# Attention with sinks: both tiles' scores in a row, their products two slots later, and the PSUM banks dealt out as four, two and two

## The chip, the core and the metric

The program runs on one core of one Trainium2 chip. The metric is the device time of one execution in microseconds (us), taken as the median of the runs. The engines go by the names of the profile: PE is TensorE (its weight loads are PEld), DVE is VectorE, ACT is ScalarE, POOL is GpSimd, SP is SyncE. Each engine takes its own queue of instructions in order; engines wait for one another by semaphores.

## The reference

Sixteen layers of a model follow one another on a tensor of 16 sequences, 256 tokens and 128 channels. The change concerns one layer, `L2_attn_b`, an attention with sinks followed by a mixture of experts, and of it only the attention:

```python
q = apply_interleaved_rope(q, cos, sin) * SCALE      # 16 heads of 64
k = apply_interleaved_rope(k, cos, sin) * SCALE      # 4 heads of 64, repeated 4 times
scores = jnp.einsum('bquh,bkuh->buqk', q, k)
scores = jnp.where(jnp.abs(pos[:, None] - pos[None, :]) <= 128, scores, NEG)
combined = jnp.concatenate([scores, sink], axis=-1)  # one sink per head
probs = softmax(combined)[..., :-1]
out = jnp.einsum('buqk,bkuh->bquh', probs, v)
return jnp.einsum('buqh,uhm->bqm', out, Wo) + bo
```

An RMS norm stands before it and another behind it.

## The kernel before

All 4096 tokens lie in SBUF with channels on the partitions, in 8 chunks of 512 tokens (two sequences each). `window_attention` is one stage of the program; its work is written out by hand in a loop over slots `n`, and the instructions of each engine keep the order in which this loop names them.

A *unit* is `(c, side, b, it, jt)`: chunk, half of the heads, sequence, tile of 128 queries, tile of 128 keys. There are 128 units, 16 per chunk, 8 per side. The two units of one query tile (`jt` 0 and 1) follow each other; I call them a pair. A side has four pairs, and the work of a pair takes two slots, a double slot. The steps, in the order in which a unit passes them:

- `prepare` (with `roped` and `moved`) makes the queries and keys of a side while the units of the side before run. For each of five parts (k, and four groups q0 to q3 of 512 columns) PE projects into a bank, ACT evicts it with its bias into `raw`, POOL multiplies by the sine (`t2`); one double slot later `moved` multiplies `raw` by the cosine and shuffles `t2` on DVE (L3191, L3192), and POOL adds the two. The first double slot of a side projects k and q0, the second q1 and q2, the third q3, the fourth none. In the third and fourth of every other side the chunk's values are made as well (`v`).
- `score`: PE multiplies keys by queries for two half sets of heads into two banks, on 64 rows of the array each; ACT takes the exponential into `pt`.
- `masked`: for unequal tiles DVE multiplies `pt` by the mask `far`; at the second unit of a pair POOL adds the pair's two `pt` into `both`.
- `weigh` (L3259): PE multiplies the weights by the values, 8 matmuls per unit on 32 columns of the array each, into the bank `po`, and at the second unit `both` by ones into the bank `pd`, which gives the sums.
- `inverse` and `divide`: ACT takes Ln of the sums with the sinks added and Exp of minus that (`rd`); DVE multiplies `po` by `rd` into `ot`.
- `out`: PE multiplies a finished side's `ot` by the output weights, four matmuls into one bank; DVE adds the result to `h` (`ha` in the profile).
- `before` and `after` are the norms of a chunk, spread over three slots each: a matmul for the mean, one for the variance, then scaling on DVE.

The loop puts `score(n)` at the head of slot n, then `masked(n - 1)` and what earlier slots left over for now (`due`: `inverse` one slot behind the products, `divide` one behind that, and the maxima `peaks`). An odd slot ends with `weigh` of units n - 3 and n - 2. An even slot ends with `prepare`, then `out`, then `before` and `after`; `prepare` begins with `moved`, and so the rotation of q3 stands in front of `out` in DVE's queue:

```python
if n % 2:
    for i in (n - 3, n - 2):
        if 0 <= i < len(units):
            weigh(i, n)
    continue
i, step = divmod(n + 8, 8)
if 0 <= i < 2 * NCH:
    prepare(i, step // 2, n)
i, rest = divmod(n - 14, 8)
if rest == 0 and 0 <= i < 2 * NCH:
    out(i)
```

The eight PSUM banks are dealt out by `share(s=4, o=4)`: four, taken in turn, for scores, projections, values, `out` and norms; four for the pairs `po` and `pd`, so that two pairs' sums can stand at once. Matmuls and the helpers `act`, `tt`, `gt` have one line each (L504, L528, L531 on DVE, L534 on POOL), so groups are told apart by the tiles' names.

Of the kernel before, what the change touches and what calls it, by code (L numbers as in the profile page):

```python
# [11 lines left out]
F32, BF16, I32 = mybir.dt.float32, mybir.dt.bfloat16, mybir.dt.int32  # L12
# [5 lines left out]
P = 128  # L18
# [3 lines left out]
NCH = NT // CH  # L22
# [1627 lines left out]
class Fast(Net):  # L1650
# [1509 lines left out]
    def window_attention(self, w, h, n1, ns2):  # L3160
# [3 lines left out]
        with ExitStack() as st:  # L3164
            p1 = self.stage(st, "w1", 1)
# [11 lines left out]
            def roped(n, g, s, t1):  # L3177


                pa = self.bank("s")  # L3180
                self.mm(pa, w["W" + n][:, g * P : g * P + P], n1[:, s])
                raw = p2.tile([P, CH], F32, tag="raw", name="raw", bufs=4)
                t2 = p2.tile([P, CH], F32, tag="t2", name="t2", bufs=4)
                self.act(raw, pa, AF.Identity, bias=w["b" + n][:, g : g + 1])
                self.gt(self.bt(t2), self.bt(raw), self.twice(w["sin"]), ALU.mult)
                pending.append((t1, raw, t2))
# [8 lines left out]
            def later(slot, f, *args):  # L3195
                due.setdefault(slot, []).append((f, args))

            def prepare(i, step, slot):

                c, side = divmod(i, 2)  # L3200
                s = self.chunk(c)
                while pending:
                    moved()
                if step == 0:
                    qs[i] = p2.tile([P, 4, CH], F32, tag="q", name="q")
                    ks[i] = p2.tile([P, CH], F32, tag="k", name="k")
                    roped("k", side, s, ks[i])
                    later(("last", slot + 4), self.peak, WINDOW + side, 1, c, ks[i])
                for g in ((0,), (1, 2), (3,), ())[step]:
                    roped("q", 4 * side + g, s, qs[i][:, g])  # L3210
                    later(("last", slot + 4), self.peak, WINDOW + side, 0, 4 * c + g, qs[i][:, g])
                if side == 0 and step > 1:
                    pv = self.bank("s")
                    v = p1.tile([P, 2, T], F32, tag="v", name="v", bufs=4)
                    for k in range(2):
                        t = 2 * step - 4 + k
                        self.mm(pv[:, k * T : k * T + T], n1[:, c * CH + t * P : c * CH + t * P + P], w["Wv"])
                        vs[c, t] = v[:, k]
                    self.tt(v, self.bt(pv), w["bv"][:, None, :].broadcast_to([P, 2, T]), ALU.add)
# [14 lines left out]
            def masked(n):  # L3234

                c, side, b, it, jt = units[n]
                if it != jt:
                    pp = pts[n].rearrange("p r h t -> p (r h) t")
                    self.tt(pp, pp, w["far"][:, it * P : it * P + P][:, None, :].broadcast_to([P, 8, P]), ALU.mult)
                if jt:  # L3240
                    both[n] = p2.tile([P, 2, 4, P], F32, tag="both", name="both")
                    self.gt(both[n], pts[n - 1], pts[n], ALU.add)

            def weigh(n, slot):
                c, side, b, it, jt = units[n]
                if jt == 0:
                    sums[0] = self.bank("o"), self.bank("o")
                pt = pts.pop(n)
                po, pd = sums[0]


                for dh in range(3 if jt else 2):
                    if dh == 2:
                        pt = both.pop(n)
                    for r in range(4):
                        half, hh = divmod(r, 2)
                        d = (2 * side + half) * 64 + 32 * dh
                        at = dh % 2 * T
                        nc.tensor.matmul(  # L3259
                            (pd if dh == 2 else po)[32 * r : 32 * r + 32, at : at + T],  # L3260
                            self.ones64[:, :32] if dh == 2 else vs[c, 2 * b + jt][:, d : d + 32],
                            pt[:, half, 2 * hh : 2 * hh + 2].rearrange("p h t -> p (h t)"),
                            start=dh == 2 or (jt == 0 and dh == 0), stop=dh == 2 or (jt == 1 and dh == 1), skip_group_check=True,
                        )
                if jt:
                    later(slot + 1, inverse, n, po, pd, slot + 2)

            def inverse(n, po, pd, slot):
                side = units[n][1]
                rd = p2.tile([P, 2, P], F32, tag="rd", name="rd")  # L3270
                for h2 in range(2):
                    self.act(rd[:, h2], pd[:, h2 * P : h2 * P + P], AF.Ln, bias=es[:, side, h2 : h2 + 1])
                self.act(rd, rd, AF.Exp, scale=-1.0)
                later(slot, divide, n, po, rd)

            def divide(n, po, rd):
                c, side, b, it, jt = units[n]
                if (b, it) == (0, 0):
                    ots[2 * c + side] = p2.tile([P, 4, CH], F32, tag="ot", name="ot")
                i0 = b * T + it * P  # L3280
                self.tt(
                    ots[2 * c + side][:, :, i0 : i0 + P].rearrange("p (d h) t -> p d h t", d=2),
                    po.rearrange("p (d h t) -> p d h t", d=2, h=2), rd[:, None].broadcast_to([P, 2, 2, P]), ALU.mult,
                )

            def out(i):
                c, side = divmod(i, 2)
                pz = self.bank("s")
                ot = ots.pop(i)
                for g in range(4):  # L3290
                    at = (4 * side + g) * C
                    self.mm(pz, w["Wof"][:, at : at + C], ot[:, g], start=g == 0, stop=g == 3)
                hs = h[:, self.chunk(c)]
                if side:
                    self.tt(hs, hs, pz, ALU.add)
                else:
                    self.stt(hs, pz, w["bo"], hs, ALU.add, ALU.add)

            held = {}

            def before(c, i):

                s = self.chunk(c)
                if i == 0:
                    held["sq"] = self.centre_step(p1, self.x[:, s], h[:, s], "s", square=True)
                elif i == 1:
                    held["rs"] = self.spread_step(p1, held["sq"], "s", twice=True)
                else:
                    r1, r2 = held["rs"]
                    self.stt(n1[:, s], h[:, s], w["ns1"], r2, ALU.mult, ALU.mult)  # L3310
                    self.tt(h[:, s], h[:, s], r1, ALU.mult)

            def after(c, i):

                s = self.chunk(c)
                if i == 0:
                    held["sq"] = p1.tile([P, CH], F32, tag="nsq", name="nsq", bufs=2)
                    self.act(held["sq"], h[:, s], AF.Square)
                elif i == 1:
                    held["rs"] = self.spread_step(p1, held["sq"], "s")  # L3320
                else:
                    self.stt(n1[:, s], h[:, s], ns2, held["rs"], ALU.mult, ALU.mult)

            with self.share(s=4, o=4), self.tc.manual_schedule():
                self.logs()
                for n in range(-14, len(units) + 16):
                    if 0 <= n < len(units):
                        score(n)
                        later(n + 1, masked, n)
                    for f, args in (*due.pop(n, []), *due.pop(("last", n), [])):  # L3330
                        f(*args)
                    if n % 2:
                        for i in (n - 3, n - 2):
                            if 0 <= i < len(units):
                                weigh(i, n)
                        continue
                    i, step = divmod(n + 8, 8)
                    if 0 <= i < 2 * NCH:
                        prepare(i, step // 2, n)
                    i, rest = divmod(n - 14, 8)  # L3340
                    if rest == 0 and 0 <= i < 2 * NCH:
                        out(i)
                    c, u = divmod(n + 14, 16)
                    if u in (0, 2, 4) and c < NCH:
                        before(c, u // 2)
                    c, u = divmod(n - 24, 16)
                    if u in (0, 2, 4) and 0 <= c < NCH:
                        after(c, u // 2)
# [459 lines left out]
```

## Time and profile before

| what | value |
|---|---|
| median of 3 runs | 4373.4 us (4373.02 to 4376.56) |
| profiled execution | 4392.96 us, span 4391.2 us, mean granted PE clock 0.952 |
| whole span, busy: PE, DVE, ACT, POOL | 90%, 59%, 54%, 48% |
| the attention's stretch | about 3028 to 3500 us |
| in 3028 to 3500, busy us of 472: PE, DVE, ACT, POOL | 448.8, 381.1, 271.7, 412.4; clock 0.99 |

Busy PE is an upper reading: matmuls are pipelined and their ends are modelled, and the instructions of row tiles and column tiles run beside each other. In the timeline each row gives the start and the time of one or several instructions in a row; in brackets stands the idle time of the engine before them and what ended it. Durations overlap a little (a row's end lies up to 0.1 us behind the next row's start on the same engine), so steps are better read from start to start. A wait for several things is put down to the one that came last.

### The profile page before, as it was taken

What the parts mean: (1) busy time and instruction counts of PE and PEld (TensorE: products, weight loads), DVE (VectorE), ACT (ScalarE), POOL (GpSimd) and SP (SyncE); (2) the same over time, 40 slices, a digit from 0 to 9 for tenths busy, and PEclk for the clock granted to TensorE, in tenths of its full rate; (3) what the DMA queues carried; (4) which work ended last, traced back from release to release, by engine and by line L of the source; (5) the groups of instructions that cost most, each with busy time, mean ns of one, the idle gap of its engine ahead of it and who ended that gap; (6) DMA issues with size and microseconds to landing.
All of it is one profiled execution on the core that took longest, in us unless ns stands there. A gap on an engine that the chain in (4) does not pass through costs nothing. (4 is left out here: it accounts for less than half of the span.)

```text
span 4391.2 us, 72802 instructions
## 1 busy us (share of the span) xinstructions
PE 3966.2 (90%) x28390; PEld 2202.4 (50%) x28390; DVE 2605.3 (59%) x4455; ACT 2376.1 (54%) x4549; POOL 2119.4 (48%) x1776
## 2 busy tenths in 40 slices
PE   7899999999899999995989969887999899899978
PEld 3455455466355445543975549643333344355333
DVE  4764566364366377456336643564888788386374
ACT  6665466444766456553447634445555554675442
POOL 4653355232455255315433334466998789521251
PEclk8999999999999999997999979998999999999989
DMA  1800000000000000001940029200000000000000
GB/s 59 332 1 1 11 1 1 19 1 1 19 1 1 1 3 1 1 0 49 310 162 10 15 88 326 86 18 16 1 1 1 3 1 1 15 2 18 6 0 20
DMA packets 78400, 176.36 MB, mean 40 GB/s; under 512 B 12606, under 2 KB 39108, under 8 KB 77920
## 3 DMA queue, kind: packets, MB, share of 16 engines
q1 hardware_dynamic: 65568, 148.40, 9.8%
q0 software_dynamic: 9120, 18.51, 1.2%
q8 instruction: 227, 3.72, 0.4%
q10 hardware_dynamic: 3360, 4.72, 0.3%
q14 instruction: 125, 1.02, 0.1%
HBM read 118.28 MB, written 54.20 MB: 39 GB/s over the span
## 5 line engine op out<-in xcount | busy, mean ns | idle before, releaser
L528 ACT ACTIVATE pt<-ps 128x512 f32<-128x512 f32 (+1 forms) x896 | 423.1, 537 | 408.1 <-PE ps L504 406.8
L504 PE MATMUL ps<-hb,w 128*128 128x512 f32 (+1 forms) x960 | 468.9, 623 | 5.4 <-issue 3.3
L531 DVE TENSOR_TENSOR t<-ps,tab 128x512 f32<-128x512 f32 x512 | 319.3, 683 | 196.1 <-ACT sq L528 191.3
L504 PE MATMUL ps<-w,hb 128*128 128x512 f32 (+2 forms) x896 | 415.1, 576 | 13.6 <-DVE t L531 11.3
L534 POOL TENSOR_TENSOR t<-t,ss 128x1024 f32<-128x1024 f32 x128 | 243.7, 1904 | 306.8 <-ACT ss L528 197.7
L534 POOL TENSOR_TENSOR t<-t,t 128x512 f32<-128x512 f32 x256 | 320.5, 1275 | 13.2 <-PE ps L504 10.1
L504 PEld LDWEIGHTS ps<-hb,w 128*128 128x128 f32 (+1 forms) x960 | 183.6, 196 | 273.5 <-issue 247.3
L531 DVE TENSOR_TENSOR u<-u,ps 128x384 f32<-128x384 f32 (+1 forms) x206 | 121.8, 595 | 277.8 <-ACT u L528 131.2
L534 POOL TENSOR_TENSOR nsq<-ha 128x512 f32<-128x512 f32 x112 | 123.2, 1100 | 314.1 <-ACT ha L528 297.3
L504 PE MATMUL ps<-nsq,ct 128*128 128x512 f32 x368 | 209.5, 654 | 53.9 <-POOL nsq L534 35.0
L528 ACT ACTIVATE pt<-pt 128x768 f32<-128x768 f32 (+1 forms) x160 | 169.5, 1060 | 154.6 <-DVE pt L531 154.6
L2199 POOL DMA_INDIRECT back<-y,x x142 | 139.1, 980 | 184.2 <-ACT y L528 90.2
L504 PE MATMUL ps<-qkt 64*128 64x192 f32 (+1 forms) x2048 | 216.2, 326 | 11.8 <-ACT pt L528 11.8
L504 PE MATMUL ps<-u,w 128*128 128x512 f32 (+1 forms) x448 | 218.8, 612 | 8.0 <-POOL u L534 8.0
L504 PE MATMUL ps<-ot,w 128*128 128x512 f32 x448 | 211.1, 604 | 15.2 <-POOL ot L534 6.9
L504 PE MATMUL ps<-xt,w 128*128 128x128 f32 x1704 | 219.8, 279 | 1.5 <-ACT xt L528 1.5
L504 PEld LDWEIGHTS ps<-qkt 64*128 64x128 f32 x2048 | 153.1, 188 | 133.3 <-ACT qkt L528 51.5
L504 PEld LDWEIGHTS ps<-w,hb 128*128 128x128 f32 x896 | 147.4, 192 | 139.4 <-issue 110.7
L531 DVE TENSOR_TENSOR pt<-ps,w 128x384 f32<-128x384 f32 (+1 forms) x320 | 171.2, 576 | 75.6 <-PE ps L504 72.2
L3705 POOL DMA_INDIRECT rows<-out,idx x128 | 126.4, 988 | 174.6 <-ACT out L528 125.6
L528 ACT ACTIVATE u<-ps,w 128x512 f32<-128x512 f32 x160 | 107.2, 685 | 186.3 <-PE ps L504 183.5
L531 DVE TENSOR_TENSOR pt<-pt,w 128x1024 f32<-128x1024 f32 (+1 forms) x96 | 181.1, 1886 | 42.3 <-ACT pt L528 42.3
(362 smaller groups left out, 9127.2 us busy)
## 6 DMA issues: line engine op xcount, KB each, us to landing
w<-in_moe_x SPq DMA_DIRECT2D x142, 533.0 KB
rows<-t SPq DMA_DIRECT2D x64, 520.0 KB
x<-rows SPq DMA_DIRECT2D x142, 65.0 KB
w<-in_local_f SPq DMA_DIRECT2D x8, 659.5 KB
y<-back ACTq DMA_DIRECT2D x16, 256.0 KB
y<-back SPq DMA_DIRECT2D x16, 256.0 KB
w<-in_local_f SPq DMA_DIRECT2D x4, 658.5 KB
back<-y,x POOLq DMA_INDIRECT x142
```

The source lines that it names most:

```text
L504: self.nc.tensor.matmul(out, lhsT, rhs, start=start, stop=stop)
L528: self.nc.scalar.activation(out, in_, func, **kw)
L531: self.nc.vector.tensor_tensor(out, a, b, op)
L534: self.nc.gpsimd.tensor_tensor(out, a, b, op)
L2199: nc.gpsimd.indirect_dma_start(views[i], bass.IndirectOffsetOnAxis(ap=x[:, C : C + 1].bitcast(I32), axis=0), y, None, bounds_check=2 * NT ...
L3705: nc.gpsimd.indirect_dma_start(views[(c * 2 + k) * 4 + t], bass.IndirectOffsetOnAxis(ap=idx[:, k, t : t + 1], axis=0), out[:, k, t], None,)
```

## The change

The loop goes by double slots. Each one scores both units of a pair in a row, masks the pair of the double slot before, and multiplies the pair of two double slots before (`weigh(n - 4)`, `weigh(n - 3)`; it was units n - 3 and n - 2 of an odd slot n). Then come the maxima, `out`, `prepare`, and `inverse`, which now holds the division as well and belongs to the pair multiplied in the same double slot; `before` and `after` close it. `out` now stands in front of `prepare`. The banks are dealt out as four for scores, two for `po` and `pd`, and two (`f`) for all the rest.

```diff
-                pa = self.bank("s")
+                pa = self.bank("f")
...
-            def weigh(n, slot):
+            def weigh(n):
...
-                if jt:
-                    later(slot + 1, inverse, n, po, pd, slot + 2)
-
-            def inverse(n, po, pd, slot):
+                sums[n] = po, pd
+
+            def inverse(n):
+                po, pd = sums.pop(n)
                 side = units[n][1]
                 rd = p2.tile([P, 2, P], F32, tag="rd", name="rd")
                 for h2 in range(2):
                     self.act(rd[:, h2], pd[:, h2 * P : h2 * P + P], AF.Ln, bias=es[:, side, h2 : h2 + 1])
                 self.act(rd, rd, AF.Exp, scale=-1.0)
-                later(slot, divide, n, po, rd)
-
-            def divide(n, po, rd):
                 c, side, b, it, jt = units[n]
...
-            with self.share(s=4, o=4), self.tc.manual_schedule():
+            with self.share(s=4, o=2, f=2), self.tc.manual_schedule():
                 self.logs()
-                for n in range(-14, len(units) + 16):
-                    if 0 <= n < len(units):
-                        score(n)
-                        later(n + 1, masked, n)
-                    for f, args in (*due.pop(n, []), *due.pop(("last", n), [])):
+                for n in range(-14, len(units) + 16, 2):
+                    two = (n, n + 1)
+                    for i in two:
+                        if 0 <= i < len(units):
+                            score(i)
+                    for i in two:
+                        if 0 <= i - 2 < len(units):
+                            masked(i - 2)
+                    for i in (n - 4, n - 3):
+                        if 0 <= i < len(units):
+                            weigh(i)
+                    for f, args in due.pop(("last", n), []):
                         f(*args)
-                    if n % 2:
-                        for i in (n - 3, n - 2):
-                            if 0 <= i < len(units):
-                                weigh(i, n)
-                        continue
+                    i, rest = divmod(n - 14, 8)
+                    if rest == 0 and 0 <= i < 2 * NCH:
+                        out(i)
                     i, step = divmod(n + 8, 8)
                     if 0 <= i < 2 * NCH:
                         prepare(i, step // 2, n)
-                    i, rest = divmod(n - 14, 8)
-                    if rest == 0 and 0 <= i < 2 * NCH:
-                        out(i)
+                    if 0 <= n - 3 < len(units):
+                        inverse(n - 3)
                     c, u = divmod(n + 14, 16)
```

`out`, the values and the norms' matmuls take their banks from `f` in the same way as `roped`. The number of tiles `pt` (six) and `both` (two) is as it was.

More of the change, by code (lines that the diff above doesn't have):

```diff
@@ L3212, in prepare @@
                 if side == 0 and step > 1:
-                    pv = self.bank("s")
+                    pv = self.bank("f")
                     v = p1.tile([P, 2, T], F32, tag="v", name="v", bufs=4)
@@ L3240, in masked @@
                 if jt:
-                    both[n] = p2.tile([P, 2, 4, P], F32, tag="both", name="both")
+                    both[n] = p2.tile([P, 2, 4, P], F32, tag="both", name="both", bufs=2)
                     self.gt(both[n], pts[n - 1], pts[n], ALU.add)
-            def weigh(n, slot):
+            def weigh(n):
                 c, side, b, it, jt = units[n]
@@ L3287, in out @@
                 c, side = divmod(i, 2)
-                pz = self.bank("s")
+                pz = self.bank("f")
                 ot = ots.pop(i)
@@ L3304, in before @@
                 if i == 0:
-                    held["sq"] = self.centre_step(p1, self.x[:, s], h[:, s], "s", square=True)
+                    held["sq"] = self.centre_step(p1, self.x[:, s], h[:, s], "f", square=True)
                 elif i == 1:
-                    held["rs"] = self.spread_step(p1, held["sq"], "s", twice=True)
+                    held["rs"] = self.spread_step(p1, held["sq"], "f", twice=True)
                 else:
@@ L3319, in after @@
                 elif i == 1:
-                    held["rs"] = self.spread_step(p1, held["sq"], "s")
+                    held["rs"] = self.spread_step(p1, held["sq"], "f")
                 else:
                     self.stt(n1[:, s], h[:, s], ns2, held["rs"], ALU.mult, ALU.mult)
-            with self.share(s=4, o=4), self.tc.manual_schedule():
+            with self.share(s=4, o=2, f=2), self.tc.manual_schedule():
                 self.logs()
-                for n in range(-14, len(units) + 16):
-                    if 0 <= n < len(units):
-                        score(n)
-                        later(n + 1, masked, n)
-                    for f, args in (*due.pop(n, []), *due.pop(("last", n), [])):
-                        f(*args)
-                    if n % 2:
-                        for i in (n - 3, n - 2):
-                            if 0 <= i < len(units):
-                                weigh(i, n)
-                        continue
+                for n in range(-14, len(units) + 16, 2):
[10 more added lines that the diff above has]
+                    for f, args in due.pop(("last", n), []):
+                        f(*args)
+                    i, rest = divmod(n - 14, 8)
+                    if rest == 0 and 0 <= i < 2 * NCH:
+                        out(i)
                     i, step = divmod(n + 8, 8)
```

## The prediction

> **What bounds the kernel now.** The page names no single bound: the last chain holds 3% for PE, and the work is a row of stages. The change touches one of them, so I read that stage by its own rows. It runs from about 3028 to 3500 us of the span: 472 of 4391 us. First the stretches, in columns of start:end and length, then busy us (instructions) of PE, PE's weight loads, DVE, ACT and POOL, then granted clock and DMA:
>
> ```profile
> 3195.00:3224.00 29.00, 27.78 (x216) 11.27 (x213) 23.85 (x30) 14.78 (x32) 26.17 (x15) 1.00 0.01 1
> 3224.00:3253.00 29.00, 28.12 (x215) 11.01 (x214) 24.31 (x32) 18.79 (x41) 25.92 (x14) 1.00 0.00 1
> ```
>
> PE is at 96%, POOL at 90%, DVE at 83%, the clock is full and DMA is nothing. PE looks like the bound. The waits of the stage and the order of time say otherwise:
>
> ```profile
> ACT pt L528 <- PE ps L504: 188.2, 84, 6.4
> PEld ps L3259 <- POOL both L534: 21.9, 16, 3.5
> PE ps L3259 <- POOL both L534: 14.2, 16, 3.0
> PE ps L504 <- POOL q L534: 7.7, 14, 1.0
> ```
>
> PE waits for POOL 14 times for `q`, 1.0 us at most: once in every side. ("ACT pt" waits long because ScalarE has little to do.) The timeline (start, duration, engine, line, instruction) shows the place; weight loads and ACT are left out:
>
> ```profile
> 3289.44 3.70 PE L504 MATMUL ps<-ot,w 128*128 128x512 f32 x8
> ...
> 3291.84 1.15 DVE L531 TENSOR_TENSOR q<-raw,w 128x512 f32<-128x512 f32 x1
> 3292.40 2.82 POOL L534 TENSOR_TENSOR both<-pt 128x1024 f32<-128x1024 f32 x1
> ...
> 3292.92 0.74 DVE L3192 STREAM_SHUFFLE t<-t 128x512 f32<-128x512 f32 x1
> 3293.07 1.13 PE L504 MATMUL ps<-q,k 64*128 64x512 f32 x4
> 3293.55 0.67 DVE L531 TENSOR_TENSOR ha<-ha,ps 128x512 f32<-128x512 f32 x1
> ...
> 3295.18 1.72 POOL L534 TENSOR_TENSOR q<-q,t 128x512 f32<-128x512 f32 x1
> ...
> 3296.95 1.13 PE L504 MATMUL ps<-q,k 64*128 64x512 f32 x4 [0.46 <-POOL q L534]
> ```
>
> The first scores of a side need the fourth part of its queries (q3), which is rotated one double slot earlier: cosine product and shuffle on DVE, sum on POOL. At present DVE does q3 (3291.84) while the `ot,w` matmuls of `out` run, and adds `out`'s result after it (3293.55). POOL then finishes q3 at 3296.90, just too late. Going back, POOL has worked without a gap since the `both` that began at 3275.46: 21.5 us (22.4 us in the neighbouring side). So the loop of a side is PE's first scores and projections, exponentials and mask (7.7 us), then POOL's row (21.5 to 22.4). The `out` matmuls repeat every 59.45 us for two sides (3200.88 to 3260.33), 29.7 per side. PE's own sum below is 28.35.
>
> **The change, part by part.** I call the four double slots of a side A (k and q0 are projected), B (q1, q2), C (q3) and D (`out`; values too in every other side).
>
> *PE's order.* It was score, projections, score, products; it becomes both scores, products, projections. The steps from start to start in the rows: one score 1.06, both in a row 1.92 (a run of eight score instructions, 3475.78 to 3477.70), products 2.30, two projections 1.92, three 2.77, `out` 3.63 and 0.85 for values. Before: A 2x1.06+2.30+1.92 = 6.34, B 7.19, C 6.34, D 8.05 (+0.43 mean for values) = 28.35. After, with 1.92 for 2.12: 27.55. That is 0.8 us per side, 12 us over 15 sides. It counts only where PE binds.
>
> *Products two slots later.* `both` is ready nearly a slot before its products; the 36 us of waits for it (21.9+14.2, largely PE and its loads counted twice) go. Late next is what follows.
>
> *ACT's and DVE's order.* In a double slot ACT now does four exponentials, the slot's `raw` evictions, and behind them Ln, Ln, Exp of the same slot's sums; DVE does mask, peaks, `out`'s add, rotations, values, and last the division. The listing of the changed kernel's instructions shows just this order on DVE in D: mask, two peaks, add to `ha` (waits for PE), q3's product, shuffle, division. So q3, which the next scores need, is queued behind `out`'s matmuls. POOL's order is unchanged.
>
> *Banks: four for scores as before, two for sums (were four), two for the rest.* The next products must now wait for the division before them. Row first: products to Ln 2.43 (3495.43 to 3497.86), Ln to division 1.11 (3299.09 to 3300.20), division 0.60: 4.14 from the start of the products, 1.84 past their end. The scores in between take 1.92, so with nothing in the way the wait is nothing; with `raw` and rotations in the way it is what the timeline below gives, 0.9 to 1.5 per side.
>
> [...]
>
> *Two banks for the rest.* B and the D of half the sides use more; the third matmul of B needs q1's eviction, 1.17+0.57 = 1.74 after the start, and comes up at 1.7: nothing.
>
> **One side, worked through.** 0 is when POOL has finished q3. From the rows: a matmul's reader starts 0.43 per instruction + 0.32 after its start (3490.74 to 3494.47 for `out`); raw 0.57; DVE mask 1.14 to 1.61, peak 0.6, q product 1.08, shuffle 0.62, k product 0.61, values and `out` add 0.6.
> - A: scores to 1.92, products to 4.22, k and q0 to 6.14. Raw of q0 6.25 to 6.82, Ln to Exp 7.93, division 8.53.
> - B: scores to 8.06; products wait 0.5 for the division, 8.55 to 10.85; projections to 13.6. Raw of q2 ends 13.45, division 15.16. DVE's mask of B stands behind A's division and ends at 9.7 to 10.1; then POOL's row begins.
> - C: scores to 15.5, products to 17.8, projections to 19.7. DVE: mask 16.8, peaks 18.0 (q0 is summed by 16.6), q1 19.7, q2 21.4, values 22.0 in every other side, division 22.0 or 22.6.
> - D: scores to 21.6; products wait 0.4 or 1.0, 22.05 or 22.65 to 24.35 or 24.95; `out`'s reader 3.73 later, 28.1 or 28.7; add, q3's product and shuffle 2.3 more: 30.4 or 31.0; POOL's sum 1.26 (alone) to 2.25 (rows), 1.7 taken (the 3295.18 row): 32.1 or 32.7.
>
> The side takes 32.4 by this path. POOL's own path agrees: 9.9 + 21.5 to 22.4 = 31.4 to 32.3. Against 29.7 that is +2.7 us. `out` and q3 meet in D in 14 slots (the changed kernel's and the present one's `ot,w` rows with projections behind them: 3082.50 to 3467.74): 14x2.7 = 38. At the stage's start, PE now waits up to 3.0 for `both`, which goes, while the divisions cost about as much: 0. At its end the last two pairs of products, now back to back, stand in row for the division: +2. Sum +40. The next stage needs this one's output, so it all counts. Profiled execution: 4392.96+40 = 4433; the median of the runs lies 19.6 lower, 4373.4+40 = 4413.
>
> Bounds: no wait for a division at all and POOL's sum at 1.26 gives A 6.14 + B 6.99 + C 6.14 + D 1.92+2.30+3.73+2.3+1.26 = 30.8, +1.1 per side, +15: 4389. Upwards, DVE's q product takes 2.2 and the mask 2.1 in rows where they meet POOL (3276.48, 3273.22): one of each more in C, +1.6 per side: 4436.
>
> **The rivals.**
> 1. *DVE free of POOL, about no change (8%).* With POOL idle while DVE waits, q3's product would cost what k's does (0.61). 30.8 becomes 30.3, +8 and less what the start of the stage saves (5.1 us of `both` waits there): 4376. For it: k's 0.68 row. Against: all 59 q products took 1.12 or more.
> 2. *PE binds, faster (6%).* If q3 is ready when PE has done D, a side is 27.55: 15x2.15 = 32 less, 4341. It decides where q3's sum ends before 28 instead of 32.4: `out`'s add would have to find its bank 4 us earlier or q3 be ahead of it. For it: PE's 96%. Against: DVE takes its queue in order, and 28.35 of PE does not explain 29.7 today.
> 3. *Collisions in C and D, much slower (16%).* Every two-input DVE step and POOL sum of C and D at its long row (mask +0.5, two q products +1.1 each): 35.1 per side, 14x5.4+2 = 78: 4451.
>
> The forecast itself has 70%, with 4389 to 4436 as its own range.
>
> **How the numbers follow.** 4413 is the forecast. The range 4384 to 4446 leaves out rivals 1 and 2 and some two fifths of rival 3: about 20%. About 0.2% (8.7 us) is what a measurement of this kernel tells from no change. Slower takes the forecast and rival 3: 0.86; same 0.08; faster 0.06.
>
> **What would show it.** Right: in each D, DVE idle 1 to 2 us before the add to `ha` for PE; PE idle 3 to 4 us before the first score of a side, released by POOL's `q` (14 times, 45 to 55 us in all); waits of PE for `both` gone; some of PE for `ot` (0.4 to 1.0 each); `out` rows 64 to 66 us apart for two sides. Wrong: rows 55 to 60 apart, or PE waiting mostly for `ot`, which would be the banks and not DVE's order.

## The result and the profile after

The changed kernel takes 4439.3 us (median of 4 runs, 4436.6 to 4440.15) where the kernel before takes 4373.2 (4 runs): 1.0152 times as long, 95% interval 1.0134 to 1.0169. The forecast was 4413.0: the sign was right, the loss is 66 us instead of 40. The time lies above the forecast's own range (4389 to 4436) and inside the wide one (4384 to 4446).

The spans of the two profiled executions differ by 47 us only (4438.2 and 4391.2). In that of before the stages ahead of the attention took 20 us more: its first scores of queries by keys stand at 3029.16, those of after at 3009.43. From these first scores to the last `out` of the stage it is 472.7 us before (to 3501.87) and 538.8 after (to 3548.22): +66.1, the whole difference of the medians.

Where in the stage? The chain of rows `ps<-ot,w` gives it: first scores to the first full `out` row +1.7 us, the 13 sides behind that +57.8 (385.24 to 443.03, that is 29.63 to 34.08 per side), the last side but one +6.4, the last +0.2.

The two stretches answer to those shown of before (start:end and length, busy us of PE, weight loads, DVE, ACT, POOL, granted clock):

```profile
3235.30:3269.60 34.30, 29.82 (x221) 12.38 (x217) 24.20 (x33) 17.89 (x38) 25.46 (x15) 0.90 0.00 1
3269.60:3303.50 33.90, 29.82 (x222) 12.31 (x218) 24.34 (x31) 17.57 (x38) 25.88 (x15) 0.95 0.00 0
```

DVE and POOL do the same work in a longer time. PE is busy for 29.8 us a side instead of some 28, though its work had become 0.8 us shorter, and the clock is no longer 1.00. The waits of the stage:

```profile
DVE ot L531 <- ACT rd L528: 128.0, 33, 8.5
PE ps L504 <- POOL q L534: 69.3, 15, 8.4
```

PE's waits for `both` are all but gone (1.4 us in two places, 0.1 in the 12 sides read below). Its waits for `q` have grown from 7.7 to 69.3 us, 8.4 of it at the stage's start. DVE now waits 128 us for `rd`, at the division. The groups of PE between the `out` rows of 3064 and 3475 (12 sides; the last column is idle time and what ended it) say that nothing else holds PE up there, the sums' two banks included:

```profile
L504 PE MATMUL ps<-q,k 64*128 64x512 f32 x384 | 111.9, 707 | 51.5 <-POOL q L534 51.5
L3259 PE MATMUL ps<-pt,v 128*32 128x256 f32 x1536 | 101.3, 408 | 0.0
```

That is 51.5 / 12 = 4.3 us of idle time per side. Before it was 14.8 us in 13 sides, 1.1 each. But a side has grown by 4.45, and PE's own work had been shortened by 0.8, so 4.3 - 1.1 - 0.8 = 2.4 explains only a part. The mean of a score instruction (707 ns, 641 before) points at the rest. One side in order of time:

```profile
3239.03 0.69 DVE L531 TENSOR_TENSOR ha<-ha,ps 128x512 f32<-128x512 f32 x1 [0.95 <-PE ps L504]
3239.64 1.80 DVE L531 TENSOR_TENSOR q<-raw,w 128x512 f32<-128x512 f32 x1
...
3242.16 1.26 POOL L534 TENSOR_TENSOR q<-q,t 128x512 f32<-128x512 f32 x1 [1.27 <-DVE t L3192]
3243.48 3.78 PE L504 MATMUL ps<-q,k 64*128 64x512 f32 x8 [4.48 <-POOL q L534]
...
3253.86 0.69 DVE L531 TENSOR_TENSOR ot<-ps,rd 128x512 f32<-128x512 f32 x1 [7.43 <-ACT rd L528]
3253.98 1.93 PE L3259 MATMUL ps<-pt,v 128*32 128x256 f32 x32
3254.46 1.22 DVE L531 TENSOR_TENSOR pt<-pt,w 128x1024 f32<-128x1024 f32 x1
3255.73 0.61 PE L3259 MATMUL ps<-both,ct 128*32 128x256 f32 x8
3255.85 2.65 POOL L534 TENSOR_TENSOR both<-pt 128x1024 f32<-128x1024 f32 x1 [1.26 <-DVE pt L531]
...
3276.91 1.26 POOL L534 TENSOR_TENSOR q<-q,t 128x512 f32<-128x512 f32 x1 [1.27 <-DVE t L3192]
```

Three things are to be seen. DVE waits 0.95 for `out`, adds it, and only then rotates q3. PE stands idle for 4.48 until POOL has summed q3; then its eight score instructions take 3.78 us, where the same eight take 1.99 in other double slots. And the mask of A's pair stands behind A's division, for which DVE has waited 7.43; POOL's row begins with the `both` of that pair, 12.4 us into the side (11.6 in the neighbouring one), and ends 22.3 us later with the next q3. It has one gap, the last line's: POOL waits 1.27 for q3's shuffle on DVE, so in D it is DVE's order that comes last.

The granted clock in small stretches fits the slow scores (behind the five busy times stand the clock, then the DMA's share and GB/s):

```profile
3241.10:3243.40 2.30, 0.00 (x0) 0.00 (x0) 2.30 (x5) 0.00 (x0) 1.24 (x1) 0.65 0.00 0
3243.40:3247.20 3.80, 3.72 (x10) 1.20 (x10) 2.99 (x4) 1.08 (x2) 1.22 (x2) 0.50 0.00 0
3247.20:3250.10 2.90, 2.90 (x42) 1.37 (x40) 0.00 (x0) 1.09 (x2) 1.16 (x1) 0.76 0.03 6
...
3275.30:3278.20 2.90, 0.00 (x0) 0.00 (x0) 2.90 (x6) 0.00 (x0) 1.60 (x2) 1.00 0.00 0
3278.20:3280.90 2.70, 2.67 (x8) 0.71 (x8) 1.65 (x2) 1.09 (x2) 1.48 (x1) 0.71 0.00 0
3280.90:3284.10 3.20, 3.20 (x43) 1.47 (x41) 0.00 (x0) 1.08 (x2) 0.88 (x1) 0.71 0.00 0
```

In other stretches of the same trace the clock is 1.00 from 3236.00 to 3241.70, 0.50 from 3241.80 to 3248.60 and 1.00 from there to 3251.00; in the second side it is 1.00 from 3274.00 to 3279.10, 0.50 from 3279.40 to 3282.70 and 1.00 from 3283.00 to 3286.00. So the first side has 6.8 us at 0.50, the second 3.3. PE is busy for 5.1 and 3.3 us of these. If half of that is lost, it is 2.6 and 1.7 us, an estimate of 2.1 per side on the mean.

### The profile page after: what moved, and what is told of

It is laid out like the page before. It is cut to its first block, busy times and chain, and to the rows that moved or that the text cites. A ratio compares the mean times of both kernels' runs of the same rounds, so it can differ in the third digit from the quotient of the medians.

```text
span 4438.2 us, 72941 instructions
## 1 busy us (share of the span) xinstructions
PE 3975.5 (90%) x28390; PEld 2208.4 (50%) x28390; DVE 2596.8 (59%) x4455; ACT 2376.6 (54%) x4549; POOL 2103.5 (47%) x1776
## 5 line engine op out<-in xcount | busy, mean ns | idle before, releaser
L531 DVE TENSOR_TENSOR ot<-ps,rd 128x512 f32<-128x512 f32 (+1 forms) x208 | 135.8, 653 | 217.1 <-ACT rd L528 217.1
L504 PE MATMUL ps<-q,k 64*128 64x512 f32 x512 | 149.8, 710 | 78.5 <-POOL q L534 78.5
L504 PEld LDWEIGHTS ps<-qkt 64*128 64x128 f32 x2048 | 153.1, 188 | 134.2 <-ACT qkt L528 51.5
```

Of the source, the lines that this page charges most:

```text
L504: self.nc.tensor.matmul(out, lhsT, rhs, start=start, stop=stop)
L531: self.nc.vector.tensor_tensor(out, a, b, op)
```

## The experiments

Two theories stood against each other for the part that the forecast lacked. **Clock**: PE falls to half speed after each wait of some 4 us (3.78 us for scores of 1.99), and 2 us per side are lost by that alone. **Order**: the sides are long because of the order on DVE and POOL alone, and slow scores are a by-product that costs nothing, since POOL's row sets the side. For the part that was forecast it is open which order matters: `out`'s addition ahead of q3 on DVE, or the division ahead of the mask. And the banks had to be separated from both. Times before differ by chip (4393.5 and 4395.7 us in the first eight runs, 4374.4 in the last four), so kernels are compared by their ratio to the kernel before on the same chip.

### Is it the clock?

**a3: work for PE in the gap.** Behind `out`, in 14 sides, four matmuls whose result nobody reads:

```diff
+                    if rest == 0 and 0 <= (n - 14) // 8 < 2 * NCH - 2:
+                        pf = self.bank("s")
+                        for g in range(4):
+                            self.mm(pf, w["Wof"][:, g * C : g * C + C], w["Wof"][:, :CH])
                     if 0 <= n - 3 < len(units):
                         inverse(n - 3)
```

> The changed kernel with four more 128x512 matmuls (3.4 us, result used by nobody) behind out in each of the 14 sides, in the gap in which PE waits for q3. Theory 'slow after idling' (PE's matmuls run at half speed for a while after a gap of 4 us: eight score instructions took 3.7 us instead of 1.92): with the gap filled they take 1.92 again, 1.6 to 2.4 us per side less although PE does more, 4405 to 4418. Theory 'they are slow for another reason' (operands or banks still in use, the order of score and products): the same time within 5 us, 4434 to 4444, or later if the filler gets in the way.

Measured: 1.0087 (1.0068 to 1.0105), less than the changed kernel with more work in it. The stage takes 509.9 us (3028.88 to 3538.79), 28.9 less than the changed kernel's. Its timeline and its clock:

```profile
3248.33 3.60 PE L504 MATMUL ps<-w 128*128 128x512 f32 x8
3252.99 1.99 PE L504 MATMUL ps<-q,k 64*128 64x512 f32 x8 [1.07 <-POOL q L534]
...
3262.90 2.64 POOL L534 TENSOR_TENSOR both<-pt 128x1024 f32<-128x1024 f32 x1 [1.26 <-DVE pt L531]
...
3283.96 1.27 POOL L534 TENSOR_TENSOR q<-q,t 128x512 f32<-128x512 f32 x1 [1.27 <-DVE t L3192]
```

```profile
3248.50:3252.90 4.40, 3.42 (x8) 1.16 (x7) 4.37 (x6) 0.00 (x0) 3.12 (x2) 1.00 0.00 0
3252.90:3254.90 2.00, 1.91 (x8) 0.69 (x8) 1.97 (x3) 0.75 (x2) 0.03 (x1) 1.00 0.04 8
```

From `out` to the next scores it is 8.20 us here (3244.79 to 3252.99) and 8.19 without the filler (3235.29 to 3243.48). So the filler costs nothing, and what it changes is the clock: 1.00 in both rows, and the scores take 1.99. A side takes 32.05 us (13 sides, 3083.96 to 3500.56) instead of 34.08. With the clock at 1.00, 2.0 us per side are gone, and POOL's row did not swallow them: in A everything waits for PE's scores and products, POOL's row too. That row begins 10.0 us into the side here (3262.90 against 3252.93, the end of the last q3) instead of 12.4, and is as long as before (22.3).

**b3: the control.** The same four matmuls in the kernel before, behind its `out`.

> A control: the kernel before with four unused 128x512 matmuls behind out in 14 sides. Where PE never idles long in a side, the filler is only work: 1.7 us of it per side, of which the idle time before the first scores (7.7 us in all) hides some: 14 x 1.7 = 24 less 0 to 8, +16 to +24 us, ratio 1.0035 to 1.0055. Rival (the filler helps by something else than the clock, such as the turn of the score banks): not above 1.001.

Measured: 1.0089 (1.0072 to 1.0106), +39 us. The expected price was too low by half: the filler of four is eight instructions in the profile and takes 3.5 us (its row starts at 3234.03, the next scores at 3237.55), where the expectation reckoned 1.7. With the right size, 14 x 3.5 = 49 less the idle time before the first scores and some of that for `both` (together 1.1 a side before, 0.4 here), 10, is 39. The clock of the kernel before is 1.00 already (3079 to 3485), and there the filler is paid. That leaves the clock, and not the turn of the score banks, as what a3 gained by.

**a4: half of the filler**, two matmuls (1.7 us, and again not the 0.85 of the expectation).

> The changed kernel with two unused 128x512 matmuls (0.85 us of PE) behind out in 14 sides, half of the earlier filler; the output is unchanged. Theory (PE's clock drops to half after an idle stretch somewhere between 2 and 3.1 us long, and a side that starts at full clock leaves the next one a shorter stretch): half the filler is enough, the eight score instructions take 1.99 us again at a granted clock of 1.00, ratio 1.007 to 1.011, about that of the filler of four. Rival (it was the amount of work that mattered, or the stretch stays above 3 us): most sides keep 3.7 us scores at 0.50, ratio 1.012 to 1.017.

Measured: 1.0121 (1.0104 to 1.0138), at the lower end of what the rival expected, with an interval that reaches into the other's. The gaps are 2.4 and 2.8 us now, and the same gap leads to different scores:

```profile
3075.88 1.99 PE L504 MATMUL ps<-q,k 64*128 64x512 f32 x8 [2.66 <-POOL q L534]
...
3141.63 3.17 PE L504 MATMUL ps<-q,k 64*128 64x512 f32 x8 [2.36 <-POOL q L534]
...
3209.01 1.99 PE L504 MATMUL ps<-q,k 64*128 64x512 f32 x8 [2.36 <-POOL q L534]
```

In the second the clock is 1.00 up to the scores and 0.61 in the 3.2 us from 3141.60; in the third it is 1.00 in the 2 us from 3209.00. So the runs show no single length from which the clock falls: it fell behind one gap of 2.36 us and not behind another. c3, below, has scores of 1.99 us behind 1.83 us and of 3.78 behind 3.12. Why one gap counts and the next doesn't is not shown here.

**a5: the changed kernel once more**, unaltered, as the base for the last group.

> The changed kernel once more, unaltered, as the base of the other runs of this group. Every theory: 1.0135 to 1.017 of the time before, out rows about 68 us apart per two sides, and the granted clock at 0.50 in the first score instructions behind each long wait for q.

Measured: 1.0143 (1.0126 to 1.0159), with scores of 2.68 to 3.79 us behind the gaps of 4.05 us and more, and `out` rows some 68 us apart, as expected.

### Which order makes q3 late?

**a1: `out`'s addition behind the rotation.** `out` returns its addition, and the loop calls it behind `prepare`:

```diff
-                    if rest == 0 and 0 <= i < 2 * NCH:
-                        out(i)
+                    added = out(i) if rest == 0 and 0 <= i < 2 * NCH else None
                     i, step = divmod(n + 8, 8)
                     if 0 <= i < 2 * NCH:
                         prepare(i, step // 2, n)
+                    if added:
+                        added()
```

> The changed kernel with one thing put back: DVE adds out's result to h after q3's rotation and the values, not ahead of them; PE's order, ACT's and the banks stay. Theory 'POOL's row' (q3 comes late mainly because POOL's gapless work on B, C and D begins 12 us into the side instead of 7.7; the queueing behind out costs POOL only the 1.27 us for which it idles before q3's sum): 1.3 us per side less, and somewhat more if PE wakes sooner, 4405 to 4425. Theory 'DVE's order' (the prediction's path through D, where q3 stands behind out's matmuls): the wait of 4 us in each of 14 sides goes, and with it the slow matmuls behind it: 4365 to 4385.

Measured: 1.0144 (1.0126 to 1.0161), a miss for both theories (4405 to 4425 and 4365 to 4385 are 1.007 to 1.012 and 0.998 to 1.003), and no gain that can be told from the changed kernel. The gap shrinks a little, from 4.1 to 4.5 down to 3.2 to 4.1 us, and most sides still start with scores of 2.70 to 3.79 us:

```profile
3284.18 2.80 POOL L534 TENSOR_TENSOR both<-pt 128x1024 f32<-128x1024 f32 x1
...
3286.94 1.26 POOL L534 TENSOR_TENSOR q<-q,t 128x512 f32<-128x512 f32 x1
3288.25 3.78 PE L504 MATMUL ps<-q,k 64*128 64x512 f32 x8 [3.21 <-POOL q L534]
```

DVE's shuffle of q3 ends at 3285.43, but POOL, whose row started late in A, is at work on `both` until 3286.98 and sums q3 only then. The order that the forecast put first is not enough by itself. But the ratio hides what it is worth: the two sides whose scores took 1.99 us (3158.58, 3223.77) take 31.4 us from `out` to `out` (3150.82 to 3182.22, 3215.99 to 3247.41), where a3's sides of the same kind, with the values behind `out`, take 32.3 (3212.50 to 3244.79). The others, with the slower scores, take 33.1 to 34.3.

**c1: the division behind the next double slot's mask.** Ln and Exp stay where they are; the division moves to the next double slot, behind `masked` and ahead of `weigh`.

```diff
+                    if 0 <= n - 5 < len(units):
+                        divide(n - 5)
                     for i in (n - 4, n - 3):
                         if 0 <= i < len(units):
                             weigh(i)
```

> The changed kernel (1.0152 of before) with one thing on DVE moved: the division of a pair stands behind the mask of the next double slot instead of ahead of it; PE's and ACT's order and the banks stay. Theory 'mask behind division': in A, DVE idles 7.4 us for the division, with the mask of A's pair queued behind it, and so POOL's row of B, C and D begins 12.4 us into the side (7.7 before). With the mask done in that idle time the row begins at the end of POOL's two sine products, 1.3 to 1.6 us earlier: 1.3 to 2.5 us per side less, 1.007 to 1.011. Theory 'two banks for sums': the division comes later still, the products wait longer for their bank, and the time is the same or longer, 1.014 to 1.025.

Measured: 1.0113 (1.0096 to 1.013), a little over the first range. Between 3100 and 3460 PE now waits 6.4 us for the division, which it did not in the changed kernel, and 35.5 for `q`.

**c2: A's own pair masked in A.** The mask of that pair, and POOL's `both`, move ahead of A's `prepare` and so ahead of A's division:

```diff
                     for i in two:
-                        if 0 <= i - 2 < len(units):
+                        if n % 8 != 2 and 0 <= i - 2 < len(units):
                             masked(i - 2)
...
+                    for i in two:
+                        if n % 8 == 0 and 0 <= i < len(units):
+                            masked(i)
                     i, step = divmod(n + 8, 8)
```

> The changed kernel with the mask and the pair sum of A's own pair done in A, ahead of the projections' work, in the time in which DVE and POOL idle there (7.4 and 3.7 us); everything else stays. Theory 'mask behind division' (POOL's row starts late): both moves out of the row, which begins up to 3.9 us sooner; the wait for q3 falls from 4.3 to what out's place in DVE's queue makes of it, some 2 us, and PE stays nearer full speed: 2 to 4.5 us per side less, 1.001 to 1.009. Theory 'late q3 is only DVE's order in D': no change, 1.014 to 1.016.

Measured: 1.0097 (1.008 to 1.0114), at or a little over the upper end of what was expected. Against the changed kernel (1.0152, and 1.0143 in a5) c1 and c2 help by some 0.3 and 0.5%; c1's interval just touches a5's. Two neighbouring sides of c2 with scores of 1.99 us take 30.8 each (3079.68 to 3141.29), where a3 has 32.05. So the mask behind the division matters, and by these rows more than `out`'s addition.

**c3: c2 and a1 together.**

> Both moves: the mask and pair sum of A in A, and out's add behind q3's rotation. The add's move alone was worth nothing measurable (1.0144 against 1.0152) since POOL's row ended later still. If the two limits lie one behind the other, as I now think, the second move pays once the first is made: a side of 28 to 29.2 us, 0.987 to 0.998 of before. If the add's place never matters: the same as the mask's move alone within 0.2%.

Measured: 1.0073 (1.0052 to 1.0093); a miss. The rows show sides of different length:

```profile
3253.39 1.99 PE L504 MATMUL ps<-q,k 64*128 64x512 f32 x8 [1.83 <-POOL q L534]
3277.16 3.70 PE L504 MATMUL ps<-ot,w 128*128 128x512 f32 x8
3284.84 3.78 PE L504 MATMUL ps<-q,k 64*128 64x512 f32 x8 [3.12 <-POOL q L534]
3311.25 3.70 PE L504 MATMUL ps<-ot,w 128*128 128x512 f32 x8
```

A side that starts behind a gap of 1.83 us takes 29.3 from `out` to `out` (3247.87 to 3277.16), nearly the expected size. One that starts behind 3.12 us takes 34.1; the clock there is 0.50 from 3284.80 to 3288.60, against 1.00 from 3253.40 to 3255.40 in the other. But even two neighbouring sides with scores of 1.99 us take 59.95 together (3217.21 to 3277.16), against 59.45 for two sides before. The expectation lacked the clock, and the order by itself brings the side near its old length and not below it.

**c4: c3 with the filler of two matmuls.**

> The kernel with A's own pair masked in A and out's addition behind the rotation, with the same two unused matmuls behind out. Theory: its sides of 34.1 us, which began with 3.78 us of scores after 3.1 us of idling, become like its sides of 29.3 us, all at 29.3 to 30.2: 14 sides times some 2 us less than the 31.5 of the same kernel without the filler, ratio 0.996 to 1.002. Rival (the two kinds of sides differ by what they compute, values in every other one, and not by the clock): they stay apart, ratio 1.006 to 1.010.

Measured: 1.0045 (1.003 to 1.0059). The clock part came out: between 3100 and 3460 all scores take 1.99 us, the gaps before them being 1.4 us or none, and the sides of 34.1 are gone:

```profile
3248.51 3.70 PE L504 MATMUL ps<-ot,w 128*128 128x512 f32 x8
...
3256.20 1.99 PE L504 MATMUL ps<-q,k 64*128 64x512 f32 x8 [1.41 <-POOL q L534]
...
3279.84 3.70 PE L504 MATMUL ps<-ot,w 128*128 128x512 f32 x8
```

Sides take 29.3 and 31.3 in turn, 30.3 on the mean. The time missed the expected 0.996 to 1.002, and the filler isn't the reason: from `out` to the next scores it is 5.54 and 7.69 us with it (3279.84 to 3285.38, 3248.51 to 3256.20), 5.52 and 7.68 in c3 without (3247.87 to 3253.39, 3277.16 to 3284.84). The expectation had all sides at 29.3 to 30.2. With scores of 1.99 us those with the values behind `out` still take 31.3, because PE waits 1.4 there for `q`; in that the rival was right, and two sides take 60.65 against 59.45 before. It is the fastest of the variants and still slower than the kernel before. A filler of one matmul was not run.

### The banks and the earlier q3

**b2: the kernel before with the banks dealt out as four, two and two**, its order untouched:

```diff
-            with self.share(s=4, o=4), self.tc.manual_schedule():
+            with self.share(s=4, o=2, f=2), self.tc.manual_schedule():
```

(and `f` for projections, values, `out` and norms, as in the change).

> The kernel before with its banks dealt out as in the changed one (four, two, two) and nothing else. In its order a division stands behind the next slot's mask, and the products of the next pair would wait for it: 1.5 to 2.3 us in each of 64 double slots if nothing hides it, 1.015 to 1.035 of before; if the projections, which now have their own banks, start earlier in return or the waits overlap those for POOL, 1.000 to 1.010. Below 1.000 would say that the deal of the banks was a gain by itself.

Measured: 1.0091 (1.0074 to 1.0107), within the second range. In the old order the division stands two slots behind the products, and with two banks the next products wait for it:

```profile
PE ps L3259 <- DVE ot L531: 30.7, 18, 6.1
```

All 18 are waits of the sums' matmuls (`both` by ones); the products by the values before them did not wait. Two more things are in the 0.9%: the norms' matmuls wait 0.85 for the eviction of `raw` in 12 places, which points at the two banks of `f`, and behind five of the six gaps of 2.9 us between 3130 and 3460 PE's next instructions are slow: from 3197.35 four score instructions take 2.08 and four projections 2.67 us, where they take 1.13 and 1.98 elsewhere. The run's mean granted clock is 0.949, that of the kernel before on the same chip 0.950 to 0.953. So the new deal of the banks costs 0.9% in the old order, the slow instructions included, and no idle time of PE in the steady part of the new one, which divides in the same double slot.

**a2 and b1: q3 projected one double slot earlier**, with k and q0, q1; q2 and q3; none; none. a2 is that in the changed kernel, b1 in the kernel before.

```diff
-                for g in ((0,), (1, 2), (3,), ())[step]:
+                for g in ((0, 1), (2, 3), (), ())[step]:
```

> The changed kernel with the projections of q0 to q3 one double slot earlier (k, q0, q1 in the first; q2, q3 in the second; none after), so that nothing in D is needed by the next side's first scores. If the late q3 carries the whole loss (its wait of 4.3 us and the 2 us by which PE's matmuls are slower behind it), a side falls from 34.1 to PE's 27.6 to 28.5 us: 4345 to 4365, below the kernel before. If the two banks for sums carry a part, waits of PE for the division stay or grow, since three evictions now stand ahead of Ln in A, 2 us in A and 1 in B: 4385 to 4400.

> The kernel before with the projections one double slot earlier in the same way. It tells what that shift is worth without the change: at most the 1.3 us per side by which its period (29.7) lies over PE's own 28.35, so 4355 to 4373. If POOL's row was its bound, the gain is there; if PE was, it is the same within 0.2%.

Measured: a2 1.0102 (1.0085 to 1.0119), b1 1.0134 (1.0117 to 1.0151). Both are misses: with 4373.4 for the kernel before, a2 was expected at 0.994 to 0.998 or 1.003 to 1.006, b1 at 0.996 to 1.000. In a2 the wait for `q` is gone, and another one is in its place, the one for two banks:

```profile
PE ps L3259 <- DVE ot L531: 51.5, 16, 4.7
```

It is the same 3 to 4 us per side in another spot. In b1, POOL's rotations crowd together and PE waits 53.5 us for `both` (15 times, up to 4.9), where the kernel before waits 14.2. There q3 had been late by 0.5 us only, so little could be won. In both runs PE is slow behind many of the new gaps: in a2 the eight `out` instructions take 5.40 us behind 3.92 (3219.48) and 3.70 behind 3.09 (3252.80); in b1 four score instructions take 2.08 instead of 1.13 behind 3.37 (3215.34). The mean granted clock is 0.948 in a2 and 0.944 in b1, 0.950 to 0.952 in the kernel before on the same chip. So neither tells what the shift is worth at a clock of 1.00.

## Why the prediction was right, and where it was short

**Direction and place: right.** PE's waits for `both` went, q3 became late, and PE stood idle once per side until POOL's `q` released the first scores. The signs it named are there in kind, but not in size: DVE idle before the addition to `ha` (0.95 and 0.5 in turn; 1 to 2 was named), the gap before the first scores 14 times (4.1 to 4.5 us in most, 61 in all; 3 to 4 and 45 to 55 were named), `out` rows 68.2 us apart for two sides (64 to 66 was named).

**One side of 32.4 us: right for a PE at full speed.** a3, whose filler lies wholly in the gap and whose scores take 1.99 us, has 32.05 per side and `out` rows 64.1 us apart for two sides. In the changed kernel itself a side takes 34.1.

**The step that failed: the first double slot.** "A: scores to 1.92, products to 4.22" took PE at full speed behind a wait of some 4 us. In 14 sides it ran at half speed there, wholly or in part (scores of 2.68 to 3.79 us), and A grew by 2 us on the mean; POOL's row moved with it (12.4 and 11.6 into the side instead of 10.0). 14 x 2.0 = 28 us of the 66, as a3 measures it: 28.9 for the stage. The remaining +37 is the forecast's +40. The trace of before held such cases at the stage's start:

```profile
3029.16 2.08 PE L504 MATMUL ps<-q,k 64*128 64x512 f32 x4 [9.86 <-POOL q L534]
```

```profile
3029.10:3031.20 2.10, 2.04 (x5) 0.54 (x5) 0.69 (x1) 0.00 (x0) 0.01 (x1) 0.50 0.00 0
```

Behind 9.86 us of idle time four score instructions take 2.08, not 1.13, at a granted clock of 0.50; behind a wait of 3.02 us for `both` (to 3057.24) the clock is 0.50 again, and the scores at 3058.91 take 2.08. The forecast rested on two stretches without a long gap, found the clock at 1.00 there, and added gaps of 4 us without asking what follows them.

**DVE's order behind `out`: named as the path, but not the only one.** The forecast noted that "POOL's own path agrees: 9.9 + 21.5 to 22.4", and a3 has 10.0 + 22.3 = 32.3 in the side shown, of which 1.27 is POOL's wait for DVE. So DVE's order comes last, and POOL's own row stands close behind it. By the sides with scores of 1.99 us, the addition's move is worth 0.9 us (a1, sides with values), the mask's 1.25 (c2), and both bring a side to 30.0 or 30.3 (c3, c4) where the kernel before has 29.7; in the ratios of a1, c2 and c3 the slow scores of the other sides (up to 3.79 us) cover a part of that.

**The wait for the sums' banks: 0.9 to 1.5 us per side forecast, none measured.** The products show 0.0 us of idle time in those 12 sides. The forecast let them wait for the division at their start. In a2 and b2, where PE does wait for the division, it is always the sums' matmuls that wait, and these come 1.75 us behind the start (3253.98 and 3255.73 in the side shown, where the division ends at 3254.55). That error and the gap's size (4.3, where 32.4 less PE's 27.55 and the bank waits had left 3.4 to 3.9) nearly cancel. In the gap, q3's product was the term that grew: it took 1.80 and 2.20 us (3239.64, 3273.99), not 1.08; POOL's sum took 1.26 and not 1.7. In b2 and a2 these waits for the division come to 30.7 and 51.5 us.

**Start and end.** Forecast 0 and +2; measured +1.7 at the start, and +6.6 for the last two sides (+4.1 in a3), where 2.7 and 2 were reckoned.

**Rivals.** PE did not bind. DVE got freer in one place, where the first rival had not looked for it: one q product in each side takes 0.68 (3263.61), though all took 1.12 or more before. That of q3 did not. The third rival's number (35.1 per side) lay nearest to the measured 34.1, but not its cause: a3, with the same order on DVE and POOL, has 32.05. The rise came from a clock that no case had (0.50 in the rows above). So it is in part luck that the measured time lies inside 4384 to 4446: the upper end was set for the third rival.

## What to carry to other kernels

When a reordering opens an idle gap on PE, price what runs after the gap too (here up to 3.79 us for scores of 1.99, behind gaps from 2.36 us on), and look for a case in the trace: the first matmuls behind any long wait. When a change of order measures as nothing, compare sides of like granted clock before calling it worthless: a1's gain was hidden that way. And a gap that can't be closed may be worth filling with idle matmuls if there is a gap to fill: b3, where PE had 1.1 us of idle time per side, paid 39 us for the same filler.

## What the hardware showed that was not expected

In the two sides of the changed kernel shown above, the granted clock of PE fell to 0.50 in the gap of 4.48 us (3241.80) or only after PE had started again (3279.40, behind a gap of 4.08 us at 1.00), and was 0.50 for 6.8 and 3.3 us. Over all runs, a side's first scores took 1.99 us (four of them 1.13) behind waits for `q` of up to 1.83 us (c3, 3253.39); the exceptions, 2.08 for four behind 0.59 in the kernel before (3058.91) and in b3 (3045.24), follow a wait of 3.02 for `both`. Behind 2.35 to 3.37 they took 1.99 us in some sides and up to 3.79 in others (2.36 in a4, 3209.01 and 3141.63; 3.37 in c2, 3117.52 and 3441.37); behind 3.41 us and more eight took 2.5 to 3.8 us each time (3.45 behind 3.41: c2, 3249.47). Elsewhere the clock also fell behind a shorter gap: behind 1.92 us before the last `out` it was 0.69 and then 0.50 in the changed kernel (from 3548.22), and 1.00 behind the same 1.92 in the kernel before (from 3501.87). So no length that is safe everywhere follows from these runs. With more work in the gap the changed kernel's stage became 28.9 us shorter (a3).
